# Routing choices taken from logits, an expert table cut in six parts, first quotients on ScalarE, and a gate block moved

## The chip, the cores and the metric

The kernel runs on one core of a Trainium2 chip. The metric is the time of one execution on the device in microseconds (us), as the median of several runs. All data are fp32.

## The reference

Eight sequences of 256 tokens with 256 channels (`x`, 8 x 256 x 256) and one condition vector of 64 for each go through four layers, each added to its input:

```python
# layer 0: conditional transformer block
x = x + attention(tc_rmsnorm(x, t, g1..), Wq, Wk, Wv, Wo)      # 16 heads of 16
x = x + silu(n @ gate_w.T) * (n @ hid_w.T) @ out_w.T            # n = tc_rmsnorm(x, t, g2..), hidden 1024
# layer 1: attention with a key mask, out projection, rms norm, scale and shift from the condition
# layer 2: a filter over the four quaternion parts and a rotation
# layer 3: mixture of experts
xn   = rms_w * (x * rsqrt(mean(x * x) + EPS))
gate = xn @ wg_W + wg_b + (genre_embed @ gg_W + gg_b)           # 8 logits a token
gate_w = softmax(gate)
topk_w, topk_i = top_k(gate_w, 2)                               # two experts a token, weights not renormalised
h1 = relu(x @ W1[e] + b1[e]); h2 = relu(h1 @ W2[e] + b2[e])     # 256 -> 512 -> 512
out = sum over the two experts of (h2 @ W3[e] + b3[e]) * topk_w
```

## The kernel before

The sequences are numbered b = 0 to 7 and go through the kernel as a pipeline. Two of them make a group g of four tiles of 128 tokens (`NTG` = 4); a group is what is routed to experts at a time. Work on one sequence is: `first_norm` (square sums, a root by Newton steps on VectorE in `rsqrt`, the quotients `xs_n` = x times root, L900 on ScalarE or L902 on another engine), `first` (flip `pt_n` on TensorE at L888 or L914, scale and shift to `xT_n` with the factors `aff`, L922 and L924, then `pk_a`, `pq_a`, `pv_a` in `qkv`), four blocks of attention, `swiglu`, a second attention, `rotate` (layer 2), `route` (choice of experts).

A *block* is a round of `scores` (`s_a`, L988, into the one buffer of four banks; ScalarE takes its exponential at L990) and the `values` of an earlier round (`o_a`, L1001, one bank), after which VectorE turns, divides and turns back (L1010 to L1018: `tu_a`, `invs`, `on_a`, `oT_a`). Between blocks stand *pieces* of other work of TensorE: for `swiglu` the gate `pg` and the hidden part `ph` (L1096, eight matmuls each; ScalarE `th` L1100, VectorE `sg` L1102 and `hT` L1104), and the down projection `pd` (L1109). At its end VectorE makes `x` (L1115), POOL makes `xs` (L1117), TensorE flips `x` to `pt_x` (L888), ScalarE copies that to `x2T` (L1122), and `pk_a`, `pq_a` and `pv_a` (L932, L962) follow with `kT_a` (L942) and `qz_a` (L946). After the second attention `py` (L1142) is copied to `o` by VectorE (L1143). All of `pt`, `pk`, `pq`, `pv`, `pg`, `ph`, `pd`, `py`, `pcount` share three banks of PSUM in turn, so a bank comes free only when the reader of the piece three before is done.

The order of TensorE's work is written out by hand: `run` takes a string of blocks, a generator of pieces, gaps that say how much other work stands behind each block, and a dict `beside` of generators that are moved on one step behind a block. VectorE and ScalarE execute in the order of the text as far as the last rounds; POOL does so only in the first part.

`route(g)` (L1190 to L1251) takes the logits `lg`, their largest `mx`, the softmax (`ls`, `pe` by ScalarE, `sm`, `si`, `prob`) and picks two experts: in `largest` an equality `eq`, a rank `rk` that makes ties unique, its largest `first`, the selection `sel`; then `both` and the running counts `seen`. `place_choices(g)` counts places on TensorE (`pk`, L1258 and L1259), finds the rows (L1262 to L1269) and lets POOL scatter a record for each token and expert (L1275). `table(key, ...)` (L1311 to L1369) turns the counts into a list of full tiles: rows on one partition of VectorE, from `count` (L1319) over `more`, `each`, `nt`, `gap`, `step` (L1326 to L1338), `end` (L1340, and seven sums one after another at L1342), `past`, `te`, `skip`, `start` (L1344 to L1353) to `first`, `todo`, `now`, `done` (L1355 to L1368). `todo` is read by the sync engine, which then fetches the expert's weights (`w_s_early`, 2180 KB, L1454) and the records (`trec`), and POOL gathers the tokens (`xg`). There is one "early" tile, from the first two groups, some "sure" tiles from three groups, and the rest.

In before, the early table is one generator step, run right behind `place_choices(1)` after the fifth block of the round i = 6:

```python
        placed = {
            2: lambda: once(compare_queries), 4: lambda: at_once(place_choices(0)),
            6: lambda: at_once(place_choices(1), first_table()),
        }.get(i, lambda: iter(()))()
```

Of the kernel before, what the change touches and what calls it, by code (L numbers as in the profile page):

```python
# [9 lines left out]
I32 = mybir.dt.int32  # L10
# [6 lines left out]
P = 128  # L17
# [475 lines left out]
def block_kernel(ctx: ExitStack, tc: tile.TileContext, a: dict, out: bass.AP):  # L493
# [543 lines left out]
    def do(parts):  # L1037
        for _ in parts:
            pass
# [5 lines left out]
    def first_norm(b):  # L1045
        s = state[b]
        s["x"] = xs_in.pop(b)
        yield from normed(
            lambda xs: s.update(xs1=xs), s["x"], f"n1_{b}", nc.gpsimd if b > 1 else (nc.vector, nc.scalar),
            (nc.scalar, nc.scalar if b else nc.vector),  # L1050
        )

# [136 lines left out]
    def route(g, x4, raw):  # L1189
        ss = wt("ss4", [P, NTG], f"ss_r3_{g}")  # L1190
        for t in range(NTG):
            junk = wt("junk", [P, D], f"junk_r3_{g}_{t}", 1)
            nc.scalar.activation(junk, x4[:, t, :], AF.Square, accum_out=ss[:, t : t + 1])
        yield
        rstd3 = rsqrt(work, ss, NTG, 1.0 / D, 1e-6, f"r3_{g}")

        def small(name, shape=(P, NTG, E)):
            return work.tile(list(shape), F32, tag=f"r_{name}", name=f"r_{name}_{g}")

        lg = small("lg")  # L1200
        for t in range(NTG):
            nc.vector.scalar_tensor_tensor(
                lg[:, t, :], raw[:, t, :], rstd3[:, t : t + 1], gconst[:, g * GB + t // (S // P), :],
                ALU.mult, ALU.add,
            )

        def over(v):
            return v.unsqueeze(2).to_broadcast([P, NTG, E])

        row = (P, NTG)  # L1210
        mx = small("mx", row)
        nc.vector.tensor_reduce(mx, lg, AX.X, ALU.max)
        ls = small("ls")
        nc.vector.tensor_tensor(ls, lg, over(mx), ALU.subtract)
        yield
        pe = small("pe")
        nc.scalar.activation(pe, ls, AF.Exp)
        yield
        sm = small("sm", row)
        nc.vector.tensor_reduce(sm, pe, AX.X, ALU.add)  # L1220
        si = small("si", row)
        nc.vector.reciprocal(si, sm)
        prob = small("prob")
        nc.vector.tensor_tensor(prob, pe, over(si), ALU.mult)
        yield


        def largest(p, name):
            top = small(f"top{name}", row)
            nc.vector.tensor_reduce(top, p, AX.X, ALU.max)  # L1230
            eq = small(f"eq{name}")
            nc.vector.tensor_tensor(eq, p, over(top), ALU.is_equal)
            rk = small(f"rk{name}")
            nc.vector.tensor_tensor(rk, eq, rank.unsqueeze(1).to_broadcast([P, NTG, E]), ALU.mult)
            first = small(f"first{name}", row)
            nc.vector.tensor_reduce(first, rk, AX.X, ALU.max)
            sel = small(f"sel{name}")
            nc.vector.tensor_tensor(sel, rk, over(first), ALU.is_equal)
            return sel, top

        sel1, w1 = largest(prob, "1")
        rest = small("rest")
        nc.vector.scalar_tensor_tensor(rest, sel1, -2.0, prob, ALU.mult, ALU.add)
        sel2, w2 = largest(rest, "2")
        both = small("both")
        nc.vector.tensor_tensor(both, sel1, sel2, ALU.add)


        for t in range(NTG):
            tt = g * NTG + t  # L1250
            nc.vector.tensor_tensor(seen[:, tt + 1, :], seen[:, tt, :], both[:, t, :], ALU.add)  # L1251
        routed[g] = both, sel1, sel2, w1, w2, small

    def place_choices(g):
        both, sel1, sel2, w1, w2, small = routed.pop(g)
        row = (P, NTG)
        pk = ps_m.tile([P, NTG, E], F32, tag="m", name=f"pk_{g}")
        nc.tensor.matmul(pk, before, both, start=True, stop=False)  # L1258
        nc.tensor.matmul(pk, ones, seen[:, g * NTG : (g + 1) * NTG, :], start=False, stop=True)  # L1259
        yield  # L1260
        place = small("place")
        nc.vector.tensor_tensor(place, pk, region.unsqueeze(1).to_broadcast([P, NTG, E]), ALU.add)  # L1262
        for n, sel, w in ((0, sel1, w1), (1, sel2, w2)):
            mine = small(f"mine{n}")
            nc.vector.tensor_tensor(mine, place, sel, ALU.mult)  # L1265
            pos = small(f"pos{n}", row)
            nc.vector.tensor_reduce(pos, mine, AX.X, ALU.add)
            posi = work.tile([P, NTG], I32, tag=f"posi{n}", name=f"posi{n}_{g}")
            nc.vector.tensor_copy(posi, pos)  # L1269
            rec = work.tile([P, NTG, 4], I32, tag=f"rec{n}", name=f"rec{n}_{g}")  # L1270
            nc.gpsimd.iota(rec[:, :, 0], [[P, NTG]], base=g * TG, channel_multiplier=1)
            nc.gpsimd.memset(rec[:, :, 2:4], 0)
            nc.vector.tensor_copy(rec.bitcast(F32)[:, :, 1], w)
            for t in range(NTG):
                sc = nc.gpsimd.indirect_dma_start(  # L1275
                    out=slots, out_offset=bass.IndirectOffsetOnAxis(ap=posi[:, t : t + 1], axis=0),
                    in_=rec[:, t, :], in_offset=None,
                )

                for other in scatters:  # L1280
                    tc.declare_no_dep(sc.ins, other.ins, reason="rows differ")
                scatters.append(sc)
        yield
# [5 lines left out]
    def row(name, shape, dtype=F32):  # L1289
        return plan.tile([1] + list(shape), dtype, tag=name, name=name)  # L1290
# [15 lines left out]
    done = row("done", [E + 1])  # L1306
    nc.gpsimd.memset(done, 0.0)

    todos = {}

    def table(key, n, n_tiles, op):  # L1311

# [4 lines left out]
        if op is ALU.is_ge:  # L1317

            nc.vector.tensor_scalar(count, pc[0:1, :], -float(SL), None, ALU.add)  # L1319
            full = full[:, :, 0:1]  # L1320
        else:
            nc.vector.tensor_copy(count, pc[0:1, :])

        nh = full.shape[2]
        more = row("more_full" if op is ALU.is_ge else "more_rest", [E, NJ, nh])
# [11 lines left out]
        nc.vector.tensor_tensor(step, done[:, 1:], done[:, 0:E], ALU.subtract)  # L1337
        nc.vector.scalar_tensor_tensor(gap, step, float(SL), gap, ALU.mult, ALU.add)  # L1338
        end = row(f"end_{key}", [E])
        nc.vector.tensor_copy(end[:, 0:1], nt[:, 0:1])  # L1340
        for e in range(1, E):
            nc.vector.tensor_tensor(end[:, e : e + 1], end[:, e - 1 : e], nt[:, e : e + 1], ALU.add)  # L1342
        past = row(f"past_{key}", [n_tiles, E])
        nc.vector.tensor_tensor(  # L1344
            past, rows["tno"][:, 0:n_tiles].unsqueeze(2).to_broadcast([1, n_tiles, E]),
# [5 lines left out]
        nc.vector.tensor_tensor(skip, past, gap.unsqueeze(1).to_broadcast([1, n_tiles, E]), ALU.mult)  # L1351
        start = row(f"start_{key}", [n_tiles])
        nc.vector.tensor_reduce(start, skip, AX.X, ALU.add)  # L1353
        first = row(f"first_{key}", [n_tiles])
        nc.vector.scalar_tensor_tensor(first, rows["tno"][:, 0:n_tiles], float(SL), start, ALU.mult, ALU.add)  # L1355
        nc.vector.scalar_tensor_tensor(
# [5 lines left out]
        if op is ALU.is_ge:  # L1362
# [3 lines left out]
            nc.vector.tensor_scalar(now, now, -1.0, float(n_tiles), ALU.mult, ALU.add)  # L1366
            nc.vector.scalar_tensor_tensor(now, now, 0.0, nt, ALU.max, ALU.min)
            nc.vector.tensor_tensor(done[:, 0:E], done[:, 0:E], now, ALU.add)  # L1368
        return end, each  # L1369

    def parts_table(each):

# [33 lines left out]
        nc.vector.tensor_reduce(expert, its, AX.X, ALU.add)  # L1406
        nc.vector.tensor_copy(todo[:, 0], expert)
        return end

    def first_table():  # L1410
        table("early", (NG - 2) * NTG, EARLY, ALU.is_ge)
        yield

    def second_table():
        table("sure", (NG - 1) * NTG, SURE - EARLY, ALU.is_ge)
        yield

    class Place:
        pass
# [348 lines left out]
    by_text = {mybir.EngineType.DVE, mybir.EngineType.Activation, mybir.EngineType.Pool}  # L1768
    with tc.manual_schedule(engines=by_text):
        keep_busy(9, "pw0")  # L1770
        do(first_norm(0))
        set_up_factors(0)
        keep_busy(4, "pw1")
        g0 = first(0)
        next(g0)
# [47 lines left out]
    for i in range(2, B - 1):  # L1823

        placed = {
            2: lambda: once(compare_queries), 4: lambda: at_once(place_choices(0)),
            6: lambda: at_once(place_choices(1), first_table()),
        }.get(i, lambda: iter(()))()
        last, rotated = rotated, rotate(i - 2)
        n1 = first_norm(i + 2) if i + 2 < B else iter(())  # L1830
# [4 lines left out]
            0: [last], 1: [last, n2], 2: [n1, n1], 3: [last], 4: [placed], 5: [r1], 6: [rotated],  # L1835
            7: [rotated, rotated],
        }
        run("bbbbbbbb", others(i - 1), gaps, beside, late_=() if i + 2 < B else (4,), starts=starts)


# [7 lines left out]
        [whole("early", n) for n in range(EARLY)] + [whole("sure", n) for n in range(SURE - EARLY)],  # L1848
        pl, "s", EARLY, near_end=(next(others_[0]) for _ in range(1)),
    )  # L1850
    next(sure)
    n2 = in_parts(B - 1, "n2")
    run("bbbvn", pieces, 3.8, {0: [n2]}, soon=2, rest=False, starts={0: [n2], 1: [n2]})

    next(pieces)
    next(pieces)
    do(in_parts(B - 3, "r1"))
    do(pieces)
    rotated = rotate(B - 3)
    pieces = others(B - 1)  # L1860
    block()

    for n in (0, 0, 1, 1, 2, 1, 2, 0):
        for _ in range(n):
            next(pieces)
        next(rotated, None)
# [1 line left out]
    next(pieces)  # L1868
    next(pieces)
    do(place_choices(NG - 2))  # L1870
    run("bbb", pieces, 20.0, {0: [second_table(), sure]})


    life_b.close()
# [29 lines left out]
    nc.vector.scalar_tensor_tensor(low, flat, INV_HIGH, low, ALU.is_lt, ALU.mult)  # L1904
    nc.vector.tensor_reduce(good, low, AX.X, ALU.add)
    nc.vector.tensor_tensor(good, good, same, ALU.add)
    end, each = table("rest", NT, NBIG - SURE, ALU.is_gt)
    pf = ps_m.tile([P, 1], F32, tag="m", name="pf")
    nc.tensor.matmul(pf, ones, good, start=True, stop=True)
    bad = plan.tile([1, 1], I32, tag="bad", name="bad")  # L1910
    badf = plan.tile([1, 1], F32, tag="badf", name="badf")
    nc.vector.tensor_scalar(badf, pf[0:1, :], -1.0, float(N_GOOD), ALU.mult, ALU.add)
    nc.vector.tensor_copy(bad, badf)
    end_p = parts_table(each)

    over = row("over", [3])
# [126 lines left out]
```

## Time and profile before

| what | value |
|---|---|
| median of three runs | 722.42 us (720.27, 722.42, 722.49) |
| profiled execution | 722.57 us; its span in the trace 720.8 us |
| mean granted clock of TensorE | 0.989 |
| busy: PE (TensorE matmul), PEld (weight load) | 700.9 us, 537.7 us |
| busy: DVE (VectorE), ACT (ScalarE), POOL (GpSimd) | 370.7, 256.4, 181.6 us |
| chain that ended last | PE 89%, DVE 6%, ACT 1%, issue 1% |
| memory read and written | 57.24 MB, 9.59 MB |

A row of the timeline reads: start and duration in us, engine, line of the kernel, operation, what it writes and reads, shape, count; in square brackets the idle time of the engine before it and what ended that. In the list of waits a row gives the engine and line that waited, the engine and line that it waited for, the sum, the number of times and the longest. In the windows the columns are the length, then busy time and instructions of PE, PEld, DVE, ACT and POOL, the granted clock, the share of DMA and GB/s. Buffer numbers are left out of names, so `x` at L1115 is `x2` of some sequence.

### The profile page before, as it was taken

The page shows a single profiled execution, that of the slowest core. Times are in us where ns is not written, and L with a number is a line of the kernel's source. Part 1 is how long each engine was busy: PE and PEld are TensorE (multiplying, and loading weights), DVE is VectorE, ACT ScalarE, POOL GpSimd, SP SyncE. Part 2 cuts the span into 40 slices and gives each one's busy share as a digit, 9 for nine tenths or more (in the row PEclk, how much of TensorE's full clock was granted, in tenths as well). Part 3 has the DMA queues.
Part 4 walks back from the last instruction along what each step waited for, and adds up shares of the span by engine and source line. Part 5 has one row for each costly group of instructions (what it writes and reads, how often), then busy time and mean ns, then how long its engine had stood idle before and what let it go on. Part 6 is the DMA issues. An engine that isn't in the chain of part 4 may idle for free.

```text
span 720.8 us, 11237 instructions
## 1 busy us (share of the span) xinstructions
PE 700.9 (97%) x4300; PEld 537.7 (75%) x4300; DVE 370.7 (51%) x1166; ACT 256.4 (36%) x411; POOL 181.6 (25%) x219
## 2 busy tenths in 40 slices
PE   8999999999999999999799999999999999999995
PEld 7567777667667667666566776788888998989884
DVE  5557435674576774577764676688321222222221
ACT  3653335345445435445234324422221212221220
POOL 4312601001001221000500106223464332433113
PEclk9999999999999999999899999999999999999998
DMA  8400000000010000010003011737584866847612
GB/s 294 160 16 15 1 1 15 1 15 16 15 60 16 9 8 1 15 59 1 3 14 126 30 60 25 286 107 228 143 274 159 226 242 187 295 154 238 188 15 34
DMA packets 26623, 67.66 MB, mean 94 GB/s; under 512 B 8120, under 2 KB 20736, under 8 KB 24128
## 3 DMA queue, kind: packets, MB, share of 16 engines
q1 hardware_dynamic: 17712, 55.20, 21.9%
q0 software_dynamic: 8560, 11.46, 7.4%
q8 instruction: 36, 0.59, 0.3%
q14 instruction: 27, 0.22, 0.1%
q10 hardware_dynamic: 288, 0.18, 0.1%
HBM read 57.24 MB, written 9.59 MB: 93 GB/s over the span
## 4 chain that ended last, share of the span: by engine, by line
PE 89%; DVE 6%; ACT 1%; issue 1%; DMA 0%; POOL 0%; POOLq 0%; DVEq 0%; ACTq 0%
PE ph_a_rest L1489 13%; PE s_a L988 9%; PE pg L1096 8%; PE o_a L1001 8%; PE ph L1096 8%; PE pd L1109 7%; PE ph_a_p L1489 5%; PE pe_a_rest L1519 4%; PE ph_s_sure L1489 4%; PE pq_a L932 4%; PE pk_a L932 4%; PE py L1024 2%; PE pe_a_p L1519 2%; PE pv_a L962 2%; PE py L1142 2%; PE pv_a L954 2%
## 5 line engine op out<-in xcount | busy, mean ns | idle before, releaser
L990 ACT ACTIVATE pe_a<-s_a 128x2048 f32<-128x2048 f32 x64 | 120.2, 1877 | 115.6 <-PE s_a L988 115.4
L988 PE MATMUL s_a<-qz_a,kT_a 32*128 32x512 f32 x512 | 74.1, 647 | 0.8 <-DVE qz_a L946 0.4
L1489 PE MATMUL ph_a_rest<-h_a_rest,w_a_rest 128*128 128x256 f32 x288 | 63.7, 379 | 0.0
L1001 PE MATMUL o_a<-pe_a,va 128*32 128x256 f32 x1024 | 62.8, 386 | 0.0
L1096 PE MATMUL pg<-xT_n,gate_wT 128*128 128x256 f32 x256 | 61.9, 385 | 0.0
L1096 PE MATMUL ph<-xT_n,hid_wT 128*128 128x256 f32 x256 | 61.5, 383 | 0.0
L1001 PEld LDWEIGHTS o_a<-pe_a,va 128*32 128x32 f32 x1024 | 30.3, 111 | 41.3 <-issue 25.1
L1489 PEld LDWEIGHTS ph_a_rest<-h_a_rest,w_a_rest 128*128 128x128 f32 x288 | 54.1, 190 | 7.0
L1109 PE MATMUL pd<-out_wT,hT 128*128 128x256 f32 x256 | 59.2, 383 | 0.0
L1096 PEld LDWEIGHTS ph<-xT_n,hid_wT 128*128 128x128 f32 x256 | 47.8, 190 | 13.0 <-DVE y L1068 3.0
L1096 PEld LDWEIGHTS pg<-xT_n,gate_wT 128*128 128x128 f32 x256 | 47.5, 190 | 12.7 <-issue 3.2
L1109 PEld LDWEIGHTS pd<-out_wT,hT 128*128 128x128 f32 x256 | 47.7, 190 | 12.3 <-issue 3.2
L1500 DVE TENSOR_SCALAR h_a_rest<-ph_a_rest,w_a_rest 128x256 f32<-128x256 f32 x36 | 17.4, 484 | 73.5 <-PE ph_a_rest L1489 72.5
L1069 POOL TENSOR_TENSOR xy<-y,x 128x512 f32<-128x512 f32 x8 | 10.1, 1268 | 147.3 <-DVE y L1068 92.4
L1498 ACT ACTIVATE h_a_rest<-ph_a_rest,w_a_rest 128x256 f32<-128x256 f32 x36 | 17.1, 474 | 77.3 <-DVE h_a_rest L1500 77.3
L1010 DVE STREAM_TRANSPOSE tu_a<-o_a 128x512 f32<-128x512 f32 x32 | 22.8, 713 | 38.6 <-PE o_a L1001 38.6
L1275 POOL DMA_INDIRECT slots<-rec,posi x32 | 31.4, 982 | 40.8 <-DVE r_mine L1265 30.8
L1533 POOL DMA_INDIRECT out<-ye_a_rest,trec_a_rest x18 | 28.5, 1581 | 39.1 <-ACT ye_a_rest L1531 30.0
L1102 DVE SCALAR_TENSOR_TENSOR sg<-th,pg 128x512 f32<-128x512 f32 x32 | 21.9, 685 | 28.2 <-ACT th L1100 28.2
L988 PEld LDWEIGHTS s_a<-qz_a,kT_a 32*128 32x128 f32 x512 | 20.4, 184 | 18.9 <-issue 12.5
L1100 ACT ACTIVATE th<-pg 128x512 f32<-128x512 f32 x32 | 19.0, 593 | 40.8 <-PE pg L1096 40.7
L1489 PE MATMUL ph_a_rest<-xt_a_rest,w_a_rest 128*128 128x256 f32 x144 | 32.6, 379 | 0.0
(353 smaller groups left out, 1177.4 us busy)
## 6 DMA issues: line engine op xcount, KB each, us to landing
w_a_rest<-in_experts SPq DMA_DIRECT2D x9, 2180.0 KB, 9.4
w_a_p<-in_experts SPq DMA_DIRECT2D x5, 2180.0 KB, 9.0
w_s_sure<-in_experts SPq DMA_DIRECT2D x4, 2180.0 KB, 10.2
w_s_early<-in_experts SPq DMA_DIRECT2D x1, 2180.0 KB
mod<-mod_rows SPq DMA_DIRECT2D x8, 256.0 KB, 3.1
tokens<-x SPq DMA_DIRECT2D x4, 512.0 KB, 2.9
out<-x SPq DMA_DIRECT2D x4, 512.0 KB, 3.8
x<-in_x SPq DMA_DIRECT2D x7, 256.0 KB, 2.7
```

Of the source, the lines that this page charges most:

```text
L932: nc.tensor.matmul(pp[:, c, :], w[:, k, c * P : (c + 1) * P], xT[:, k, :], start=k == 0, stop=k == KC - 1)
L988: nc.tensor.matmul(sc[:, j], kT[r, c, kc * P : (kc + 1) * P], qz[r, c], start=True, stop=True)
L990: nc.scalar.activation(pe, sc, AF.Exp)
L1001: nc.tensor.matmul(o[32 * i : 32 * i + 32, qd, :], va[:, kc, 8 * c + 4 * qd + i].rearrange("p a d -> p (a d)"), pe[:, 2 * qd + i // 2, i % ...
L1010: nc.vector.transpose(turned.rearrange("p q j a d -> p (q j a d)"), o.rearrange("p q s -> p (q s)"))
L1096: nc.tensor.matmul(ps[:, j, :], w[:, k, o : o + P], yT[:, k, :], start=k == 0, stop=k == KC - 1)
L1102: nc.vector.scalar_tensor_tensor(sg, th, 1.0, pg, ALU.add, ALU.mult)
L1109: nc.tensor.matmul(pd[:, t, :], hT[:, c, t * P : (t + 1) * P], out_w[:, c, :], start=c == 0, stop=c == HID // P - 1)
L1275: sc = nc.gpsimd.indirect_dma_start(out=slots, out_offset=bass.IndirectOffsetOnAxis(ap=posi[:, t : t + 1], axis=0), in_=rec[:, t, :], in_o ...
L1489: nc.tensor.matmul(ph[:, c - c0, 0:many], w[:, o : o + P], src[:, k, 0:many], start=k == 0, stop=k == n_in - 1,)
L1519: nc.tensor.matmul(pos[q][0:p, q, :], h2[:, k, q * p : (q + 1) * p], w[:, o : o + D], start=k == 0, stop=k == MC - 1,)
L1533: ad = nc.gpsimd.indirect_dma_start(out=out[0 : reach(n), :], out_offset=bass.IndirectOffsetOnAxis(ap=rec[0:p, q, 0:1], axis=0), in_=y[0:p ...
```

## The change

1. `first_norm(0)`: both tiles of the first quotients are made by ScalarE, and the factors `aff` are put between root and quotients.
2. `route` chooses from the logits themselves: the first choice is where `lg` equals `mx`, then that one is lowered by `MASKED` and the second is taken likewise. The softmax is left to the end: `ls` gets a ninth column, the second largest minus the largest, and exponential, sum, reciprocal and second weight are taken in `place_choices`, the exponential on ScalarE behind the matmuls `pk`. `route` yields at other places.
3. `table` yields four times, so it has five stretches of work and is moved on along two steps of the pipeline: `count` after the sixth block of round 6, `more` to `gap` after the seventh, `end` after the eighth; `past` to `start` and `first` to `done` in the next step. The matmul `pcount_early` moves behind `pt_x`. The mod transfer of the last sequence now stands ahead of the load of `todo` on the sync engine, and POOL's `xs` of b = 6 ahead of its gathers.
4. In the step of b = 6 one piece `pg` of the last sequence is put between the flip `pt_x` and the projection `pk_a`, with its `th` ahead of `kT_a` and its `sg` ahead of `qz_a`. The pieces behind are dealt out anew among the blocks, and `pk` of group 2 comes after eight pieces of `pd` instead of four.

The tables for sure and rest tiles do the same as before.

```diff
-            lambda xs: s.update(xs1=xs), s["x"], f"n1_{b}", nc.gpsimd if b > 1 else (nc.vector, nc.scalar),
+            lambda xs: s.update(xs1=xs), s["x"], f"n1_{b}", (nc.scalar, nc.scalar) if b == 0 else (nc.vector, nc.scalar) if b == 1 else nc.gpsimd,
...
         mx = small("mx", row)
         nc.vector.tensor_reduce(mx, lg, AX.X, ALU.max)
-        ls = small("ls")
-        nc.vector.tensor_tensor(ls, lg, over(mx), ALU.subtract)
-        yield
-        pe = small("pe")
-        nc.scalar.activation(pe, ls, AF.Exp)
-        yield
-        sm = small("sm", row)
-        nc.vector.tensor_reduce(sm, pe, AX.X, ALU.add)
-        si = small("si", row)
-        nc.vector.reciprocal(si, sm)
-        prob = small("prob")
-        nc.vector.tensor_tensor(prob, pe, over(si), ALU.mult)
         yield
...
-        sel1, w1 = largest(prob, "1")
+        sel1 = largest(lg, mx, "1")
         rest = small("rest")
-        nc.vector.scalar_tensor_tensor(rest, sel1, -2.0, prob, ALU.mult, ALU.add)
-        sel2, w2 = largest(rest, "2")
+        nc.vector.scalar_tensor_tensor(rest, sel1, -MASKED, lg, ALU.mult, ALU.add)
+        yield
+        mx2 = small("mx2", row)
+        nc.vector.tensor_reduce(mx2, rest, AX.X, ALU.max)
+        sel2 = largest(rest, mx2, "2")
...
+        ls = small("ls", (P, NTG, E + 1))
+        nc.vector.tensor_tensor(ls[:, :, 0:E], lg, over(mx), ALU.subtract)
+        nc.vector.tensor_tensor(ls[:, :, E], mx2, mx, ALU.subtract)
+        routed[g] = both, sel1, sel2, ls, small
...
         nc.tensor.matmul(pk, ones, seen[:, g * NTG : (g + 1) * NTG, :], start=False, stop=True)
+
+        pe = small("pe", (P, NTG, E + 1))
+        nc.scalar.activation(pe, ls, AF.Exp)
         yield
...
+            sm = small("sm", row)
+            nc.vector.tensor_reduce(sm, pe[:, :, 0:E], AX.X, ALU.add)
+            w1 = small("si", row)
+            nc.vector.reciprocal(w1, sm)
+            w2 = small("w2", row)
+            nc.vector.tensor_tensor(w2, pe[:, :, E], w1, ALU.mult)
...
-        do(first_norm(0))
+        n1 = first_norm(0)
+        next(n1)
+        next(n1)
         set_up_factors(0)
+        do(n1)
...
-            6: lambda: at_once(place_choices(1), first_table()),
+            6: lambda: at_once(place_choices(1)),
...
+        if i == B - 2:
+
+            early = table("early", (NG - 2) * NTG, EARLY, ALU.is_ge)
+            for t in (5, 6, 7):
+                beside[t].append(early)
...
-    next(sure)
     n2 = in_parts(B - 1, "n2")
-    run("bbbvn", pieces, 3.8, {0: [n2]}, soon=2, rest=False, starts={0: [n2], 1: [n2]})
+    run("bbbvn", pieces, 3.8, {0: [n2], 2: [early], 3: [early]}, soon=2, rest=False, starts={0: [n2], 1: [n2]})
 
     next(pieces)
     next(pieces)
     do(in_parts(B - 3, "r1"))
+    rotated, last = rotate(B - 3), others(B - 1)
+    next(last)
     do(pieces)
-    rotated = rotate(B - 3)
-    pieces = others(B - 1)
+    do(early)
+    next(sure)
+    pieces = last
     block()
 
-    for n in (0, 0, 1, 1, 2, 1, 2, 0):
+    for n in (0, 0, 1, 1, 1, 2, 2):
```

In `table` a `yield` is put behind `count`, behind `gap`, behind `end` and behind `start`.

## The prediction

> **What bounds the kernel now.** The page first: which engine is busy, and what the chain that ended last ran through.
>
> ```profile
> PE 700.9 (97%) x4300; PEld 537.7 (75%) x4300; DVE 370.7 (51%) x1166; ACT 256.4 (36%) x411; POOL 181.6 (25%) x219
> PE 89%; DVE 6%; ACT 1%; issue 1%; DMA 0%; POOL 0%; POOLq 0%; DVEq 0%; ACTq 0%
> PEclk9999999999999999999899999999999999999998
> ```
>
> TensorE works for 700.9 of 720.8 us, and the change takes no matmul away, so all there is to win are its waits and stretches at half clock. An average of 51% for DVE says nothing about the places where it is full. So next the waits of PE, the engine line for line:
>
> ```profile
> PE pt_x L888 <- DVE o L1143: 4.0, 1, 4.0
> PE pk L1258 <- DVE r_both L1246: 1.7, 2, 1.3
> PE pt_n L914 <- DVE aff L636: 0.9, 1, 0.9
> PE pk_a L932 <- ACT x2T L1122: 0.9, 2, 0.7
> ```
>
> These four lines are 7.5 us, and each meets one part of the change. Then the busy time in windows of 10 us (PE, PEld, DVE, ACT, POOL, then the granted clock, DMA share, GB/s):
>
> ```profile
> 350.00:360.00 10.00, 5.99 (x39) 2.79 (x41) 8.86 (x49) 3.98 (x7) 7.87 (x8) 0.66 0.03 3
> 400.00:410.00 10.00, 8.91 (x44) 7.30 (x42) 7.76 (x24) 2.67 (x7) 1.26 (x1) 1.00 0.07 24
> 420.00:430.00 10.00, 8.54 (x45) 6.80 (x43) 8.42 (x38) 1.42 (x3) 0.00 (x0) 1.00 0.01 2
> ```
>
> Around 350 DVE is full, PE idles for 4 us, and the clock falls to 0.66: the wait costs twice. Last the timeline there:
>
> ```profile
> 347.94 1.26 DVE L1265 TENSOR_TENSOR r_mine<-r_place,r_sel 128x32 f32<-128x32 f32 x1
> 350.20 0.15 DVE L1319 TENSOR_SCALAR count_early<-pcount_early 1x8 f32<-1x8 f32 x1
> 354.61 0.75 DVE L1143 COPY o<-py 128x264 f32<-128x264 f32 x2
> 355.08 1.11 PE L888 MATMUL pt_x<-ident,x 128*128 128x128 f32 x4 [4.01 <-DVE o L1143]
> 356.12 2.09 PE L988 MATMUL s_a<-qz_a,kT_a 32*128 32x512 f32 x8
> ```
>
> From 350.20 to 354.6 DVE does the early tile's table, one tiny row after another; the copy that frees a bank for pt_x stands behind it. Afterwards a scores block takes 2.09 us; later, at full clock, 1.14.
>
> **Part by part** (times of the profiled execution, 722.57 us; its span is 720.8, and 722.57 lies 0.15 above the median 722.42).
>
> *First quotients on ScalarE.* The PE gap of 0.95 before pt_n at 8.49 is made by DVE's half of xs_n, 1.35 us from 6.99, and the aff behind it. ACT's half took 0.51 from 6.98; two such on ACT took 0.91 (at 225.97). So ACT ends at 7.89, aff is out of the way, pt_n starts near 7.95: 0.54 earlier, taken as **-0.5**. Bounds: 0 (ACT stretched as DVE was) and -2.1, if the shorter gap also spares the half clock from 8.5 to 11.9, where pt_n takes 1.09 (0.60 at 234.41), pk_a 2.51 (1.99 later) and six pw some 0.6 too long. The Trainium skill, "ScalarE: Activation LUTs", section "Rules for kernel authors", says to multiply on VectorE, not ScalarE, which speaks against this part. At 13.32 DVE took 0.35 for such a tile; at that price DVE would end at 7.34 with ACT's half at 7.49, and the move would lose some 0.4 instead of gaining 0.5. The 1.35 was measured in the very place, beside POOL's memsets, and it decides.
>
> *Choices from logits, group 0 (rows 219 to 235).* Removed from the path: ls, the exponential on ACT, sm, si, prob, one top. But choosing now happens earlier: 5 small rows (eq to rest, 0.22 apart) stand before hT_2, and 12 (six of 0.22, four seen in 0.77, two ls) between hT_4 and the norm's root chain, which started at 223.74. Before, sm, si, prob were there. hT_2 moves from 220.0 to 220.9, hT_4 ends near 222.9, the twelve near 225.2, so the chain is 1.5 late. Behind it, in order: ACT's xs_n, junk and th_6, DVE's sg_6, hT_6, the root chain of the next sequence, POOL's xs_n, which started at 232.11 and took 1.82 to 233.93. PE was ready for pt_n at 234.41, 0.48 later. New wait: 1.5 - 0.5, **+0.95** (0.3 if sg absorbs, 2.1 if nothing does and a POOL row meets it). The down projection reaches hT_6 half a microsecond after it is there, so it does not wait.
>
> *Group 1 (327 to 345).* The rows before hT_4 delay it by some 0.5; pd started at 336.81 and had slack for most: **+0.1** (0 to 0.3).
>
> *The table in six parts, and place_choices(1) (346 to 368).* place_choices now has 12 rows instead of 9 (sm, reciprocal, w2: 0.66 more), so it ends near 350.95, the 1.26 of r_mine included; the first o copy ends at 351.35 and pt_x starts at 351.37 instead of 355.08. From then on DVE has no pause, and I follow DVE: second copy 0.3, xT_n 0.98, root chain 2.15, the two x rows 0.88 and 0.69, raw 0.36, count 0.15 (part one), the turn, reciprocal, product and turn of a block 1.95, three rows of the rotation 1.95, part two (more to gap, 350.38 to 351.53) 1.1, qz_a 1.40: some 11.5, to 362.85. PE at full clock from 351.37: pt_x 0.66, pcount_early 0.3 (now here), s_a 1.07, o_a 1.86, s_a 1.07, pk_a 1.83, pq_a 1.73, pv_a 1.88: ready at 361.6. So scores of this sequence wait 1.25 for qz_a and start at 362.85 instead of 367.43: **-4.6**. Of that 4.0 is the stall and some 2.3 the half clock (pt_x 0.45, s_a 0.95, o_a 0.92 too long), less the new wait, the pcount and a short wait at pt_x. Bounds -3.5 (another 1.26 like r_mine on the chain) and -5.9 (no new wait). The other four parts: part three (eight rows, 1.5) lies before a turn at 370.77; DVE's gaps after it are 0.32, 0.41 and 1.67 before py is turned into y at 377.57. Part four (0.7) lies in 2.93 of idle before the turn at 395.50, parts five and six (1.45) after the o copies at 401.33, with x not started before 402.69 (idle 1.36). If this cover were gone they would cost 3.6.
>
> *Early tile's loads.* todo_early is ready near 402 rather than 354; SP loads it behind the mod transfer, which now goes first, then weights (issued 386.79 before, used at 452.88), records and POOL's gathers, which POOL does after xs. With 9 us a weight transfer they land near 410, 40 us early; the gathered tokens, used at 450.60, near 415. Nothing: 0.
>
> *Gate piece.* pg_0 of the last sequence (8 matmuls, 1.73) stands between pt_x and pk_a and fills the 0.68 that PE waited for x2T. x is 0.1 late for the table's last part; its wait of 0.42 stays. sg_0 (0.69) now stands before qz_a, which followed with some 0.2 to spare. **-0.7** (-0.5 to -0.9).
>
> *Choices, group 2 (427).* Before pk DVE ran 15 rows from 424.96 to 428.26. sm, si, prob and a top go (0.9), five more are done before hT_6, and pk now comes after eight pieces of pd instead of four. The waits 1.33 and 0.13 go: **-1.5** (-1.2 to -1.7). *Group 3 (497):* 0.33 and 0.19 go with the round trip: **-0.5** (0 to -0.8).
>
> Sum: -0.5 + 0.95 + 0.1 - 4.6 - 0.7 - 1.5 - 0.5 = -6.75, so 715.8 profiled, and **715.7** beside the median. Behind 500 PE has next to no waits, so all of it reaches the end.
>
> **Rivals.** *A, half given back:* both new waits are twice as long (pt_n 2.1, qz_a 2.5, a small DVE row stretched by 1.1 beside POOL as r_mine was: 1.26 against 0.18 at 349.61). -6.75 + 1.15 + 1.25 = -4.35: 718.1. For it: DVE is full in both places. Against: the POOL row that stretched it stays where it was.
> *B, no new waits:* the 0.95 and the 1.25 are absorbed and the start runs at full clock: -6.75 - 2.2 - 1.6 at most, some 712.7 with half of the start. Against: my count of DVE is continuous.
> *C, slower:* the inserted DVE rows are uncovered and come back as PE waits, long enough for the clock to fall. Uncovered parts +3.6, pt_n +1.15, qz_a +1.25, and 2.3 of half clock at each of the two: +10.6 - 6.75 = +3.85, 726.3. It decides once what is given back passes 6.75; the waits alone are 6.0, so it takes a drop of the clock too. What the trace has on that: 2.15 us idle in the 3.41 us up to 353.23 were followed by half clock until 360.05; 1.33 idle at 427 was not. So a wait of 0.95 or 1.25 should leave it whole, 2.1 or 2.5 not. The Trainium skill, "TensorE: Matmul & The Clock Gate", Part 1, puts the drop only after an idle window of about 3.4 us; by that neither wait could cost clock, and C would end at -0.75. The record at 353 shows a drop after less.
> *D, the removal doesn't happen:* the o copies still wait for something else than the table (py, which ended near 350.6). Only -1 of the 4.6 is left: 719.3.
>
> **How the numbers follow.** Forecast 0.70, A 0.12, B 0.10, C 0.04, D 0.04. Adding the one-sided bounds of the terms as independent gives about 2 each way (start 1.6, table 1.3, group 0 1.15), 713.5 to 717.8; widened to B and past A, so that about 2 in 10 is left out, the range is **712.5 to 718.7**. About 0.3% (2.2 us) is what a measurement can tell from no change. Faster by more: forecast, A, B and D, 0.96, less 0.04 for their slow edges: 0.92; within it: those 0.04; slower: C, 0.04.
>
> **What would show it.** Right: pt_x without a wait over 0.7, the window at 350 with the clock near 1.00, no pk behind r_both, pk_a behind no x2T; new lines pt_n <- POOL xs_n near 0.95 and s_a <- DVE qz_a near 1.25; pt_n at the start near 7.95. Wrong: half clock in the 220s to 360s, a turn or y that PE waits for between 366 and 378, or weights of the early tile among PE's waits.

## The result, and the profile after

| | before | changed |
|---|---|---|
| median | 722.45 us (720.27 to 722.76, 4 runs) | 714.86 us (713.96 to 715.89, 4 runs) |
| profiled execution, span | 722.57, 720.8 us | 713.96, 712.2 us |
| ratio | | 0.9902, 95% interval 0.9875 to 0.9928 |

The forecast was 715.7 in 712.5 to 718.7. The page of the changed kernel, its busy line and its clock:

```profile
PE 698.3 (98%) x4300; PEld 536.7 (75%) x4300; DVE 367.3 (52%) x1165; ACT 256.7 (36%) x412; POOL 182.5 (26%) x219
PEclk9999999999999999999999999999999999999998
```

TensorE's work is the same 4300 records. Its busy time is 2.6 us less, which goes with less half clock: 3.41 us of it while PE still had work, against 10.23 before. The waits of PE, on the changed kernel (sum, times, longest; left out is the 1.5 at the very start, which before has too):

```profile
PE s_a L988 <- DVE qz_a L946: 1.0, 1, 1.0
PE pt_n L888 <- POOL xs_n L902: 0.6, 1, 0.6
PE pt_x L888 <- DVE x L1115: 0.4, 1, 0.4
PE pt_x L888 <- DVE o L1143: 0.3, 1, 0.3
PE pk_a L932 <- ACT x2T L1122: 0.2, 1, 0.2
```

All four lines shown of before are gone or below 0.35 us, and two new ones lead: the two that the prediction named, at 1.0 and 0.6. The 0.4 of pt_x for x was there before. The windows around the old waits (events lie up to 8 us earlier now):

```profile
350.00:360.00 10.00, 9.54 (x79) 6.20 (x78) 9.30 (x37) 6.79 (x9) 6.65 (x7) 1.00 0.14 29
400.00:410.00 10.00, 10.00 (x50) 7.89 (x49) 8.68 (x25) 4.40 (x6) 1.55 (x2) 1.00 0.56 223
420.00:430.00 10.00, 10.00 (x59) 7.57 (x61) 5.70 (x30) 2.15 (x3) 2.95 (x3) 1.00 0.01 0
```

PE is busy 9.54 of 10 us at 350 where it was 5.99, at a clock of 1.00 where it was 0.66, and DVE is still full (9.30): the table's rows are somewhere else, not gone. They now start at 356.76, 360.58, 365.75, 388.14 and 396.91, in five pieces, not the six that the title and the prediction speak of. The window at 400 flatters: of the two waits that it held before, the 0.42 of pt_x for x still stands and lies at 399 now, just ahead of it; from 395 to 405 PE is busy 9.58. The timeline at 350:

```profile
348.45 1.26 DVE L1262 TENSOR_TENSOR r_mine<-r_place,r_sel 128x32 f32<-128x32 f32 x1
351.69 0.66 PE L888 MATMUL pt_x<-ident,x 128*128 128x128 f32 x4 [0.32 <-DVE o L1143]
363.09 1.14 PE L988 MATMUL s_a<-qz_a,kT_a 32*128 32x512 f32 x8 [0.98 <-DVE qz_a L946]
```

The flip waits 0.32 instead of 4.01 and takes 0.66 instead of 1.11. How far one kernel is ahead of the other is read best at starts of the same work in both timelines, mostly scores blocks, of which both run 64 in the same order:

| start of | before | changed | ahead by | step | forecast |
|---|---|---|---|---|---|
| first scores block | 16.54 | 14.48 | 2.06 | -2.06 | -0.5 |
| sixth scores block | 40.55 | 40.18 | 0.37 | +1.69 | none |
| scores behind pt_n of the seventh sequence | 234.94 | 235.45 | -0.51 | +0.87 | +0.95 |
| scores behind qz_a of the sixth sequence | 367.43 | 363.09 | 4.34 | -4.85 | -4.6 and +0.1 |
| down projection ahead of pk, group 2 | 425.19 | 419.99 | 5.20 | -0.86 | -0.7 |
| second scores block behind that pk | 435.83 | 428.75 | 7.08 | -1.88 | -1.5 |
| scores of the last sequence | 446.33 | 438.85 | 7.48 | -0.40 | none |
| end of the last matmul | 711.77 | 703.31 | 8.46 | -0.98 | -0.5 |

The start and what follows it at 36 us differ most from the forecast; the last three steps are each 0.4 to 0.5 larger than forecast. The experiments take up the start, the table, the gate piece, the choices and the two new waits.

### The profile page after: what moved, and what is told of

It is laid out like the page before. It is cut to its first block, busy times and chain, and to the rows that moved or that the text cites. A ratio compares the mean times of both kernels' runs of the same rounds, so it can differ in the third digit from the quotient of the medians.

```text
span 712.2 us, 11237 instructions
## 1 busy us (share of the span) xinstructions
PE 698.3 (98%) x4300; PEld 536.7 (75%) x4300; DVE 367.3 (52%) x1165; ACT 256.7 (36%) x412; POOL 182.5 (26%) x219
## 4 chain that ended last, share of the span: by engine, by line
PE 91%; DVE 5%; ACT 1%; issue 1%; POOL 1%; DMA 0%; POOLq 0%; DVEq 0%; ACTq 0%
PE ph_a_rest L1492 13%; PE s_a L988 9%; PE pg L1096 8%; PE o_a L1001 8%; PE ph L1096 7%; PE pd L1109 7%; PE ph_s_sure L1492 6%; PE ph_a_p L1492 5%; PE pe_a_rest L1522 4%; PE pq_a L932 4%; PE pk_a L932 4%; PE py L1024 2%; PE pe_s_sure L1522 2%; PE pe_a_p L1522 2%; PE pv_a L962 2%; PE py L1142 2%
```

## Experiments

**Another chip.** The first four kernels ran on another chip than all others, where before itself took 734.22 us (731.03 to 738.52). Their traces show stretches in which DVE and ACT stand still together, while PE works in bursts or stops too. In the kernel without the gate piece, near 372 us:

```profile
372.37 0.72 DVE L1010 STREAM_TRANSPOSE tu_a<-o_a 128x512 f32<-128x512 f32 x1 [6.16 <-PE pq_a L932]
372.47 1.88 ACT L990 ACTIVATE pe_a<-s_a 128x2048 f32<-128x2048 f32 x1 [7.68 <-PE pq_a L932]
```

Two engines that read different things (`o_a` and `s_a`) start 0.1 us apart after 6 and 8 us. Such stops come near 260, 372 and 450, each while POOL scatters records; the program of the first of these experiments was run again on the chip of the remaining kernels, and its trace there has none. What makes them was not found. So these four are read by steps between scores blocks away from the stops.

> The changed kernel with the early table in one piece again, behind the second placing of choices. Theory (the table is worth 4.9 of the gain, a good half of it the wait and the rest half clock): pt_x waits some 4.4 us for the o copy again (4.0 and the placing's longer chain), a half-clock record follows near 355, the 0.98 us wait of s_a for qz_a is gone, and the kernel takes 4 to 5 us more than the changed one, about 719.5. Rival (the table was hidden behind the placing of choices anyway): under 1 us more, no half clock near 355.

```diff
-            6: lambda: at_once(place_choices(1)),
+            6: lambda: at_once(place_choices(1), table("early", (NG - 2) * NTG, EARLY, ALU.is_ge)),
...
-            for t in (5, 6, 7):
-                beside[t].append(early)
...
```

736.02 us, 1.0019 of before (0.9999 to 1.0038). pt_x waits 4.22, and half clock follows at 363. From the scores block ahead of the stall to the one behind qz_a it takes 21.52 us (355.14 to 376.66). In the kernel without the gate piece, which has the table in parts, it takes 21.52 too (357.12 to 378.64), where the changed kernel took 15.28 on the other chip: as far as these two traces tell, the stop near 372 took all here that splitting the table gives. The run was repeated below.

> The changed kernel with the first quotients as before (one tile on DVE, one on ScalarE, the factors behind them). The first scores block began at 16.54 us before and at 14.48 in the changed kernel. Theory 1 (only the path to pt_n got shorter): it begins near 15.0 and the kernel takes 0.5 more. Theory 2 (the shorter wait also spared a half-clock stretch at 8.5): it begins near 16.5, and from there on 2 us are missing unless the half-clock record at 36 us of the changed kernel goes away too; with it gone 0.4 more, with it there 2.0 more.

```diff
-        n1 = first_norm(0)
-        next(n1)
-        next(n1)
+        do(first_norm(0))
         set_up_factors(0)
-        do(n1)
```

739.74 us, 1.0060 of before (1.0039 to 1.0082), with the stops in it. First scores block at 16.18, as theory 2 said; but the kernel without the gate piece, whose start is that of the changed kernel, has it at 16.46. Both reached full clock only at 10.3 and 10.9 us in these executions, and in both the first flip pt_n starts at 9.3 without a wait. So this pair of traces decides between neither theory: where the clock comes that late, the move is worth nothing. The start is taken up below, with the clock of all traces.

> The changed kernel without the gate piece between flips and projection. Theory: pk_a waits about 0.7 us for x2T again, and the step costs 0.7 to 0.9 more, about 715.7 in all. Rival (the piece only moved the wait to its sg or its bank): no more than 0.2.

```diff
     rotated, last = rotate(B - 3), others(B - 1)
-    next(last)
...
-    for n in (0, 0, 1, 1, 1, 2, 2):
+    for n in (0, 1, 1, 1, 1, 2, 2):
```

737.58 us, 1.0056 of before (1.0031 to 1.0081), stops included. The step itself is clear of them: the wait is back in the timeline,

```profile
418.04 1.99 PE L932 MATMUL pk_a<-x2T,L_WkT 128*128 128x256 f32 x8 [0.68 <-ACT x2T L1122]
```

and between the scores blocks 55 and 59 it takes 51.64 us (390.73 to 442.37) against 50.77 in the changed kernel (373.13 to 423.90): 0.87. Theory holds.

> The kernel before with nothing but the choices taken from logits. Theory (the terms add up): pt_n waits for POOL's xs_n, 0.9 lost near 235; 1.9 gained at pk near 427, 1.0 at pk near 497, the table's stall 0.4 longer; sum -1.6 to -2.4, about 720.4. Rival (the new wait at 235 and a longer chain ahead of the table's stall eat it): within 0.7 of before.

Edit: `route` and `place_choices` of the changed kernel in the kernel before. 736.94 us, 1.0029 of before (1.0006 to 1.0052). The total can't be read because of the stops, but steps away from them can. The new wait of pt_n (0.57) is there, and the wait of pk for r_both is gone. From the scores block ahead of that pk to the one behind it, it takes 17.18 us (419.88 to 437.06) against 19.06 in before (410.20 to 429.26): 1.88 less. From the last scores block to `pcount_rest`, the matmul behind the pk of group 3, it takes 33.89 (477.19 to 511.08) against 34.87 (463.44 to 498.31): 0.98 less. So the theory holds at these places, and the choices alone give both steps, with pk where it stood before.

**The remaining kernels** ran on a chip where before took 722.40 and, beside the last four, 723.51.

> The changed kernel once more, beside before on the same chip. In the last four runs before itself took 734 us, and the traces show stretches near 260, 370 and 450 us in which all engines stand still at once, beside the scatters and the mod transfer. Theory (the change gains 7.5 whatever the chip): 7 to 8.5 less than before here too. Rival (where such a stretch falls on the place that the change clears, the gain is spent there): within 3 of before, with a stop of 5 to 6 us near 370.

715.89 us, 0.9897 of before (0.9864 to 0.9930). The gain of the first comparison (0.9902) holds here. The rival was for the other chip and is not settled there: the changed kernel itself never ran on it, and the two kernels nearest to it were 0.6% slower than before.

> The kernel before, to have its trace on this chip. If the chip is like the one of the first comparison: 722, no stop of all engines. If it is like that of the last four runs: 734, stops near 260 and 450, and near 365 one that is shorter because the wait for the table overlaps it.

722.83 us; no stops. Its profiled execution (720.40) is a second look at before. Its first scores block starts at 14.91, not 16.54, and there is one half-clock record behind the table's stall, 354.1 to 357.6, instead of two windows; the stretch from the scores behind pt_n to those behind qz_a takes 131.79 us, against 132.49 in the first trace and 127.64 in the changed kernel. So the table is worth 4.15 to 4.85, by how the stall falls into the windows of the clock: in all these traces the clock changes in steps of 3.41 us or multiples of that, called windows here, and they lie differently in each execution.

> The changed kernel with the second choice of group 0 (twelve rows of DVE) moved behind the root chains of the two norms, one step later. Theory (these twelve rows make pt_n wait): the wait of pt_n for POOL's xs_n near 234 goes, and the time from the scores block at 194 to the one at 235 is 0.87 shorter than in the changed kernel. Rival (the five rows ahead of hT_2 are enough): the wait stays at 0.3 or more.

```diff
+        if i == 4:
+            beside[1] = [n2]
```

714.25 us, 0.9876 of before (0.9845 to 0.9908). No wait of pt_n; the block behind it is 0.87 earlier against the changed kernel. Theory holds, and the five rows ahead of hT_2 cost nothing.

> The changed kernel with part two of the early table behind qz_a instead of ahead of it. Theory: the wait of s_a for qz_a near 362 (0.98) goes, and the scores block there starts 1.0 earlier; nothing comes back at the turn that follows, which has 2 us to spare. Rival (part two then delays the turn and py): the 1.0 is lost again by the y row some 10 us later.

```diff
-            for t in (5, 6, 7):
-                beside[t].append(early)
+            beside[5].append(early)
+            beside[7] = [rotated, early, rotated, early]
```

712.06 us, 0.9855 of before (0.9823 to 0.9887). No wait of s_a; the block is 1.05 earlier, and 0.18 of it is lost at the next one, behind py. Theory holds but for that 0.18. The median is 3.8 below the changed kernel on this chip. 0.87 of that is the edit; for the rest, this trace is at full clock from 6.27 and has no half clock at 36, where that of the changed kernel on this chip is at full clock from 10.49 and has a record at 37.8.

> The kernel before with eleven matmuls of the identity (22 records, about 3.2 us) ahead of pt_x in the table's stall, into the scores' banks; nothing reads them. The wait for the o copy stays. Theory (the half clock behind the stall comes from PE's idleness): no half-clock record near 353, pt_x still starts behind the same copy, and from pt_x to the scores block after qz_a 1.2 us (one window) to 2 us (two) are gained, some 721 in all. Rival (DVE and not the clock sets the pace behind the stall): the record goes and nothing is gained.

```diff
+        if b == 5:
+            pw = ps_s.tile([P, 4, 2, S], F32, tag="s", name="pw_fill")
+            for _ in range(11):
+                nc.tensor.matmul(pw[:, 0, 0, 0:P], ident, ident, start=True, stop=True)
         pt = flipped(x2, f"x2_{b}")
```

722.26 us, 0.9985 of before (0.9970 to 0.9999). The timeline, with the filler in the stall:

```profile
350.82 2.62 PE L1123 MATMUL pw_fill<-ident 128*128 128x128 f32 x22
355.00 0.66 PE L888 MATMUL pt_x<-ident,x 128*128 128x128 f32 x4 [1.56 <-DVE o L1147]
355.59 1.14 PE L988 MATMUL s_a<-qz_a,kT_a 32*128 32x512 f32 x8
```

pt_x starts when it did (355.08 before), but at full clock, and from it to the scores behind qz_a it takes 10.31 us, against 11.65 and 12.35 in the two traces of before. So 1.3 to 2.0 of the table's worth is the clock, as expected, and only the rest the wait. The median is 1.25 below that of before beside it (723.51). The profiled execution gave most of its gain back: it has a new half-clock record, 428.2 to 431.6, and from the scores block behind the pk of group 2 to the next it takes 8.21 us against 6.57. That record stands behind the wait of pk for r_both, the same 1.33 us of idling that had left the clock whole in both traces of before:

```profile
420.00:430.00 10.00, 8.54 (x39) 6.43 (x39) 7.53 (x34) 2.48 (x3) 1.04 (x2) 0.91 0.00 0
```

> The changed kernel with the early table in one piece again, as before, now beside before on this chip. Theory (the table is worth 4.2 to 4.9): pt_x waits 4.3 for the o copy, a half-clock record follows near 355, s_a does not wait for qz_a, and the time is 4 to 5 above the changed kernel, near 719.5. Rival: under 1 us more.

Edit as in the first of the experiments. 720.59 us, 0.9957 of before (0.9939 to 0.9976): 4.7 above the changed kernel on this chip. Its lines:

```profile
354.62 1.11 PE L888 MATMUL pt_x<-ident,x 128*128 128x128 f32 x4 [4.32 <-DVE o L1143]
355.66 2.09 PE L988 MATMUL s_a<-qz_a,kT_a 32*128 32x512 f32 x8
```

Half clock from 354.0 to 360.9, no wait of s_a behind it. From the scores block ahead of the stall to the one behind qz_a it takes 21.34 us, against 15.28 in the changed kernel. Theory holds. In this trace, with the longer placing of choices in front, the whole table costs 6.1, more than in before and more than the 4.7 between the medians.

> The changed kernel with the router constant pgconst (sixteen records near 33 us, 8 columns each, 1.95 us) made with 64 columns of the same operand repeated; only the first 8 are read. In the changed kernel a half-clock record follows at 36 us in some executions, where this stretch falls within one window of 3.41 us. Theory (what the clock counts is work in the array, not issued instructions): no such record at any phase, clock 0.997 or so in nearly all executions whose start is at full clock, and 0.5 to 1 less in the median. Rival (64 columns are still too few, or the record has another cause): the record stays in about half of them.

```diff
-        pg = ps_m.tile([P, B, E], F32, tag="m", name="pgconst")
+        pg = ps_m.tile([P, B, E, E], F32, tag="m", name="pgconst")
+        wide = ggw.unsqueeze(1).to_broadcast([C, E, E])
...
-            nc.tensor.matmul(pg[:, b, :], cond_b[:, b, :], ggw, start=True, stop=True)
+            nc.tensor.matmul(pg[:, b, :, :], cond_b[:, b, :], wide, start=True, stop=True)
...
```

712.60 us (712.30 to 715.82), 0.9870 of before (0.9838 to 0.9903). The profiled execution has no record at 36; but its clock windows cut the stretch in two (one ends at 33.56, the stretch runs from 32.62 to 34.62), and so cut, the narrow constant leaves no record either (the kernel with part two moved has a boundary at 33.57 and none). The median is 3.3 below the changed kernel on this chip where 0.5 to 1 was expected, more than one such record is worth, so the windows fell differently as well. Neither decides for or against the theory.

> The changed kernel with all three: the second choice of group 0 behind the root chains, part two of the table behind qz_a, and the wide constant. Theory (the steps add up): no wait of pt_n near 234, none of s_a near 362, both 0.87 shorter, the half clock at 36 gone: 1.7 to 2.6 under the changed kernel, near 713. Rival (one of the moved pieces meets the other on DVE): a new wait of over 0.3 between 230 and 380.

710.87 us (710.56 to 711.17, 5 runs), 0.9832 of before (0.9812 to 0.9853): the fastest kernel here, 4 to 5 us under the changed one and 2 under what was expected. Neither new wait is in it:

```profile
230.00:240.00 10.00, 10.00 (x75) 7.34 (x74) 5.21 (x19) 2.09 (x2) 2.33 (x3) 1.00 0.00 0
360.00:370.00 10.00, 10.00 (x76) 6.96 (x69) 8.45 (x26) 3.32 (x4) 0.18 (x2) 1.00 0.00 0
```

Between the scores blocks 1 and 64 the steps against the changed kernel are 0.87, 1.05, 0.18 back, and 1.69 at 36 us; 1.74 are the two moves, the rest how the execution fell into the clock's windows, with or without help of the wide constant.

## Why the prediction was right

**The start** was forecast at -0.5 and looked like -2.06, followed by +1.69 at 36 us. What the move is worth depends on where the windows of the clock lie. Three cases are in the traces:

- Full clock only from 10.3 us on or later (one trace with the old start, three with the new): the first scores block starts at 16.2 to 17.65, and pt_n at 9.3 without a wait with either start. By these four the move is worth nothing there.
- Full clock from 5.7 to 6.3 (two old, four new): the block starts at 14.91 in both old ones (before again, and choices alone) and at 14.30 to 14.74 in the new ones, 0.2 to 0.6 earlier, as forecast. pt_n starts at 7.72 to 7.91 where 7.95 was forecast.
- Full clock from 4.8 to 5.3 (two old, two new; the first comparison is of this kind): both old ones fell to half clock at 8.3 to 8.5, behind a gap of 0.95 and 1.02 ahead of pt_n, and the block starts at 16.54 and 16.46. Neither new one fell, with gaps of 0.11 and 0.36, and it starts at 14.48 and 14.72.

The flip in before and in the changed kernel, of the last kind:

```profile
8.49 1.09 PE L914 MATMUL pt_n<-ident,xs_n 128*128 128x128 f32 x4 [0.95 <-DVE aff L636]
```

```profile
7.74 0.94 PE L914 MATMUL pt_n<-ident,xs_n 128*128 128x128 f32 x4
```

So here the shorter gap seems to have spared the half clock, which the prediction had as its bound of -2.1. With two traces of each start, and no run that holds the windows fixed, that is likely and not shown.

The +1.69 is a half-clock record from 36.0 to 39.4. In the changed kernel's trace:

```profile
32.80 1.95 PE L758 MATMUL pgconst<-small_in,cond_b 64*128 64x8 f32 x16
34.87 2.67 PE L932 MATMUL pk_a<-xT_n,L_WkT 128*128 128x256 f32 x8
37.34 2.91 PE L1024 MATMUL py<-L_WoT_turned,oT_a 128*128 128x256 f32 x8
```

pk_a took 1.96 in before. The kernel gave PE the same work there; what differs is that the stretch of tiny matmuls and the 0.12 wait behind it fell whole into one window of 3.41 us (32.57 to 35.98), while in before a boundary at 35.78 cut it. With each trace's records continued in steps of 3.41 us, this stretch lies whole (to 0.01 us) in one window in all six traces that have the record, and is cut in the six others with the narrow constant, which have none (in before again by only 0.07 us). Two steps of opposite sign made a net of -0.37. That it is near my -0.5 is luck: the record at 36 was not foreseen.

**Group 0** (+0.95): +0.87, through the chain that was followed; moving the twelve rows took exactly that away. **Group 1** (+0.1): none.

**The table** (-4.6): -4.85 and -4.15 by the two traces of before. The stall, the clock behind it (2.3 forecast; 1.3 to 2.0 by the filler) and the new wait (1.25 forecast, 0.98) were all there. The sum for DVE has a slip: the rows listed add up to 11.9, not "some 11.5", and would have made the wait some 0.4 longer. The trace has 11.3 from the start of pt_x to the end of qz_a, so the figure carried on was near for no stated reason. The other parts cost nothing: between 366 and 420 us no wait of PE is new. The early tile's weights, records and tokens never made PE wait: the weights were issued at 398.45, took 8.4 us to land and were used at 445.40. (The mod transfer of the last sequence follows them at 403.34, where the text on the change and the prediction have it first; PE waited for neither.)

**The gate piece** (-0.7): -0.86, and 0.87 when undone.

**Choices of groups 2 and 3** were the term that was mis-sized: -1.5 and -0.5 forecast, -1.88 and -0.98 measured, and the same two numbers with the choices alone. I had added up the waits that the profile lists, 1.33 and 0.13, 0.33 and 0.19. In before:

```profile
428.41 0.38 PE L1258 MATMUL pk<-r_both,before 128*128 128x32 f32 x2 [1.33 <-DVE r_both L1246]
428.92 0.41 PE L1259 MATMUL pk<-seen,ones 128*128 128x32 f32 x2
```

and in the changed kernel:

```profile
423.45 0.30 PE L1251 MATMUL pk<-r_both,before 128*128 128x32 f32 x2
423.59 0.39 PE L1252 MATMUL pk<-seen,ones 128*128 128x32 f32 x2
```

From one pair to the next it is 0.51 in before and 0.14 now, 0.37 for a listed wait of 0.13 (at 497: 0.61 and 0.14, 0.47 for 0.19). So a matmul that waits costs some 0.2 to 0.3 more here than its listed wait: it starts that much later against the one ahead than it does without a wait, and the list counts only from the modelled end of that one.

**The 0.40 of the last sequence** was not foreseen. In before s_a waited 0.41 for qz_a at 446.33, and behind that stood one row of the sure table beside POOL's scatters and its xs, in before and now:

```profile
440.14 1.89 DVE L1356 SCALAR_TENSOR_TENSOR first_sure<-done,first_sure 1x4 f32<-1x4 f32 x1
440.73 1.28 POOL L1117 TENSOR_TENSOR xs<-x,mod 128x512 f32<-128x512 f32 x1
```

```profile
433.05 0.15 DVE L1367 SCALAR_TENSOR_TENSOR first_sure<-done,first_sure 1x4 f32<-1x4 f32 x1
```

The same row of four numbers took 1.89 and 0.15. It ended within 0.05 us of POOL's `xs`, as r_mine did, whose row is shown with the prediction. In the changed kernel a copy of 128x16 took 1.36 a little later instead, beside the same row of POOL, where it made nobody wait. This is read from the traces; no experiment moved that row alone.

**The sum** was -6.75. The steps from the first scores block on, without the record at 36, are +0.87 -4.85 -0.86 -1.88 -0.40 -0.98 = -8.1 by the first trace of before and -7.4 by the second; with 0.2 to 0.6 at the start that is 7.6 to 8.7. The medians show 7.6 and 6.5. Both traces of the changed kernel have the record at 36, but four of its eight executions have a mean clock of 0.997, which leaves no room for it (it alone takes 0.0024 of the mean, and the end, where PE has run out of work, another 0.0027 in the first trace), and took 714.32 to 715.89 all the same. A late start, up to 3 us in the traces, is the likely cause for these; no trace of them is there. So part of the nearness of 715.7 to 714.86 is luck: the steps behind the start gave 1 to 2 us more than the 6.25 forecast for them (the choices 0.86 and the last sequence 0.40 of it), and the clock took it back. The rivals: A's doubled waits and C's lost cover did not come; B has both waits wrong but not the start; D's copies waited for nothing else. The rule of the Trainium skill that was weighed there ("TensorE: Matmul & The Clock Gate", Part 1: a drop only after an idle window of about 3.4 us) does not agree with the runs, here as in the prediction: 2.15 us idle, 1.95 of tiny matmuls and 0.12 idle, and 1.33 idle with the tiny matmuls behind it, were each followed by half clock when they fell into one window.

## What to carry to other kernels

Where the engine that sets the end waits for another that is busy with many tiny instructions, look for the one early consumer and cut the rest into pieces for the later idle places: here 4.5 us of table rows were worth 4 to 5, by the wait and the half clock behind it, once they stood behind the copy. Then follow the busy engine, row by row, to the next consumer; that gave both new waits to within 0.4 us, and moving just those pieces one consumer further took them away. Compare two traces by starts of the same work, not by totals: that tells what an edit did from what the clock did, whose windows lie differently in each execution.

## What was not expected of the hardware

The clock's windows lie differently against the program in each execution, and that moves the start by up to 3 us and a drop of 1.7 us in or out, as much as most parts of this change. A wait that costs no clock in one trace may do so in another, by where it falls in the windows: the wait of 1.33 for r_both in the kernel with the filler. Two tiny rows of DVE beside POOL's tensor work, r_mine and first_sure, took 1.26 and 1.89 us instead of 0.18 and 0.15. And on one chip DVE and ACT stood still for several microseconds beside the scatters; whether the change gains anything there stays open, as does whether a wider constant keeps the clock up at 36 us.
